# Layer 1's projection after its sums over edges instead of before them

## The chip, the cores and the metric

The kernel runs on one core of one Trainium2 chip. The metric is the time of one execution on the device in microseconds (us); the time before is the median of 14 runs. Engines are named as in the profile: PE is TensorE's matmul, PEld its weight load, DVE VectorE, ACT ScalarE, POOL GpSimd, SP SyncE. A line such as L589 is line 589 of the kernel before.

## The reference: what is computed

Two graph attention layers, each with a residual and a layer norm, over 3327 nodes of 1024 features. The adjacency matrix is symmetric, has ones on its diagonal and is sparse (each off-diagonal pair is drawn with a chance of 0.0024 in either direction).

```python
# layer 0: 8 heads of 128
h = x @ W0
e = leaky_relu(alpha_src[:, :, None] + alpha_dst[:, None, :], 0.2)   # per head
attn = softmax(where(adj == 0, -inf, e))
x = layernorm(x + concat_heads(attn @ h_heads))
# layer 1: one head of 1024
h = x @ W1
e = leaky_relu((h @ a1) + (h @ a2).T, 0.2)
attention = softmax(where(adj > 0, e, -9e15))
x = layernorm(x + relu(attention @ h))
```

All of it is float32.

## The kernel before, in words

Nodes are cut into 26 tiles of 128 targets (NT = 26). The kernel has a first stage and then one of two arms, chosen by a flag that the first stage computes; these inputs take the sparse arm.

**First stage (L320 to L441).** For each tile it loads rows of x and of the adjacency matrix, projects x with W0 (L415), computes the attention scores of layer 0 and writes a row of 1040 numbers for each node to DRAM (h0_d): 1024 projected features and 16 factors of the scores. It counts the edges and makes, for the first 13 tiles (LP = 13), lists of edges: for each of five blocks (EB = 5) four groups of 128 source indices (NG = 4, idx), a one-hot matrix of which of a group's 32 targets each edge belongs to (oh), and the targets' score factors (re). The lists of the other 13 tiles are made later, beside layer 0.

**Layer 0 in the sparse arm (class Layer0, L556 on).** A target tile has five steps. For each step `fetch` issues four indirect DMAs on POOL (`gather`, L513 to L521) that bring the rows of 4 x 128 edges from h0_d into one of five buffers (srcs, NS = 5). `fetch` of the next tile's step b is issued after step b of this tile, since it takes the same buffer; so gathers run a whole tile ahead. `step` makes the weights w (L580, L581) and the weighted one-hot matrices e (L583) on DVE, and sums over edges on PE: 32 matmuls of 128 columns, each for 32 targets (L589), and four small ones for the softmax's denominators (L597). A float32 matmul shows up as two records in the trace. `finish` divides, adds the residual, normalizes and stores the tile to x1_d (L612).

**Layer 1's projection (project1, L535 to L554)** is a generator: its parts are taken out one at a time by `fill`, which `step` calls after every second head, so they are written between the parts of the next tile's steps. It transposes the tile's output (eight transposes, L155, and two copies), multiplies with W1 (16 matmuls of 512 columns, L542), copies the sums to SBUF (L549), multiplies them with a1_src and a1_dst and adds up along the row (score1, L192), takes exponentials of the scores, and writes rows of 1028 numbers to h1_d (L553): 1024 features, a one, and three factors of the scores.

**Layer 1 in the sparse arm (class Target, L640 on, with Layer1, L445 on).** Again five steps a tile, with gathers of rows from h1_d. For each group, ACT (L654) and DVE (L658) make the weights es. PE sums the 1025 columns (1024 features and the one, whose sum is the denominator) in three cuts of 342, 342 and 341 columns (L664). `finish` (L462) applies the reciprocal and the Relu (L468), adds the residual, which `prepare` had loaded from x1_d (L454), normalizes and stores the output. It is called in step 2 of the next tile.

**What sets the order.** The program's order is a priority, not the order of execution: each engine's order is laid down when the program is built by a scheduler that lets later work go ahead where earlier work isn't ready by its own estimate. In the trace, L244, the start of an edge list, runs eight times between 633.7 and 709.0 us, though the program first asks for one of those lists eleven tiles later. On the chip each engine then works through its order strictly and waits at its head. Buffers are shared by tag: a tag with a number of slots hands out the next slot when its last reader is done.

```python
            while later:
                fill()
            la.finish()
```

In layer 0 this stands after the five steps of a tile (L633): what is left of the generators is written before the tile's finish, whose last line appends the tile's own projection for the next tile's steps.

Of the kernel before, what the change touches and what calls it, by code (L numbers as in the profile page):

```python
# [9 lines left out]
F32 = mybir.dt.float32  # L10
# [16 lines left out]
def kernel(  # L27
# [23 lines left out]


    nc = tc.nc
    N, D = x.shape
# [35 lines left out]
    h0_d = scratch.tile([NP, HW0], F32, name="h0_d")  # L90
    h1_d = scratch.tile([NP, HW], F32, name="h1_d")
    wd_d = [scratch.tile([P, WD], BF16, name=f"wd_d{t}") for t in range(NT)]
# [39 lines left out]
    def spread(dst, a):  # L132

        nc.sync.dma_start(dst, bass.AP(tensor=a.tensor, offset=a.offset, ap=[[0, P], [1, D]]))

    class Phase:
# [51 lines left out]
        def score1(self, ht, t):  # L188
# [6 lines left out]
            self.r1.weights(t)  # L195

        def load_a1(self):
            self.a1 = [self.pool.tile([P, D], F32, name=f"a1_{n}") for n in range(2)]
            spread(self.a1[0], a1_src)
            spread(self.a1[1], a1_dst)  # L200

# [243 lines left out]
    class Layer1:  # L445


        def __init__(self, ph, t):
            self.ph, self.t, self.src = ph, t, {}

        def prepare(self):
            self.r = self.ph.row(self.ph.r1, [self.t], 0)
            self.res = self.ph.sbuf("y", [P, D], 3, "res")
            nc.sync.dma_start(self.res, x1_d[self.t])  # L454

        def fetch(self, j):
            pass

# [15 lines left out]
    def layer1(targets, steps):  # L474
        targets[0].prepare()
        for j in range(steps):
            targets[0].fetch(j)
        for t, tg in enumerate(targets):
            tg.begin()
            for j in range(steps):  # L480
                tg.step(j)
                if t and j == min(3, steps // 2):
                    targets[t - 1].finish()
                if t + 1 < NT:
                    if j == steps // 2:
                        targets[t + 1].prepare()
                    targets[t + 1].fetch(j)
        targets[-1].finish()


    def sparse(own):
# [4 lines left out]
        for s in srcs:  # L496
            nc.vector.memset(s, 0.0)
        ph.r1 = Rows(pool, 1)
        wt = pool.tile([P, KT, D], F32, bufs=1, name="wt1")
        for k in range(KT):  # L500
            nc.sync.dma_start(wt[:, k, :], w1[k * P : (k + 1) * P, :])
        ph.load_a1()
        ph.edge_constants()
        later, listed = deque(), {}

# [28 lines left out]

        def project1(t, y):  # L535

            xT = sbuf("xT", [P, KT, P], 2)
            yield from ph.transposed(xT, y)
            acc = [bank("S", [P, HALF], "mm") for _ in range(2)]
            for k in range(KT):  # L540
                for g in range(2):
                    nc.tensor.matmul(  # L542
                        acc[g], xT[:, k, :], wt[:, k, g * HALF : (g + 1) * HALF], start=k == 0, stop=k == KT - 1
                    )
                yield
            ht = sbuf("x1", [P, HW], 2, "h1")
            nc.gpsimd.memset(ht[:, D : D + 1], 1.0)
            for g in range(2):
                nc.scalar.activation(ht[:, g * HALF : (g + 1) * HALF], acc[g], AF.Copy)  # L549
            ph.score1(ht[:, :D], t)  # L550
            for i, v in enumerate((ph.r1.a, ph.r1.b, ph.r1.nb)):
                nc.vector.tensor_copy(ht[:, D + 1 + i : D + 2 + i], v[:, t, :])
            nc.sync.dma_start(h1_d[t * P : (t + 1) * P, :], ht)  # L553
            yield  # L554

        class Layer0:  # L556
# [5 lines left out]
            def prepare(self):  # L562
                self.oh, self.re = listed.pop(self.t)
                self.ohf = sbuf("ohf", [P, NB, GT], 2)
                nc.scalar.activation(self.ohf, self.oh, AF.Copy)
                self.y = sbuf("y", [P, D], 3)
                load_rows(self.y, x, self.t)

# [33 lines left out]
            def finish(self):  # L602
                ri = sbuf("ri", [P, H], 2)
                nc.vector.reciprocal(ri, self.den)
                y = self.y
                for h in range(H):
# [4 lines left out]
                ph.layer_norm([y])  # L611
                nc.sync.dma_start(x1_d[self.t], y)  # L612
                later.append(project1(self.t, y))

# [6 lines left out]
        for b in range(EB):  # L621
            lays[0].fetch(b)
        for t, la in enumerate(lays):
            la.begin()
# [14 lines left out]

        class Target(Layer1):  # L640

            def prepare(self):
                super().prepare()
                self.oh = sbuf("oh", [P, NB, GT], 3, dt=U8)
                nc.sync.dma_start(self.oh, oh_d[self.t])

            def fetch(self, b):
                self.src[b] = gather(h1_d, HW, self.t, b)

            def step(self, b):  # L650
                s = self.src[b]
                es = sbuf("e", [P, NG, GT], 3, "es")
# [9 lines left out]
                for c in range(3):  # L662
                    for g in range(NG):
                        nc.tensor.matmul(  # L664
                            self.acc[c][g * GT : (g + 1) * GT, : CUTS[c + 1] - CUTS[c]], es[:, g, :],
                            s[:, g, CUTS[c] : CUTS[c + 1]], start=b == 0, stop=b == EB - 1,
                        )

        layer1([Target(ph, t) for t in range(NT)], EB)


# [149 lines left out]
```

## Time and profile before

| | |
|---|---|
| median of 14 runs | 2618.31 us (2603.04 to 2630.63) |
| the profiled execution | 2613.62 us |
| its span, first to last instruction | 2611.9 us |
| PE busy | 2022.8 us, 77% |
| DVE busy | 1143.6 us, 44% |
| ACT busy | 620.6 us, 24% |
| POOL busy | 1134.7 us, 43% |
| DMA | 611.67 MB, mean 234 GB/s |
| granted TensorE clock, mean | 0.854 |

The profile is a page about one execution. Its first part gives each engine's busy time; the second cuts the span into 40 slices of 65 us, with a digit of busy share for each engine, the clock that TensorE was granted and the DMA engines' share. Groups of instructions follow, by line, engine and operation, with their count, busy time, the mean time of one in nanoseconds, and the idle time of the engine just before them with what ended it. Further views answer questions on the trace: the timeline in order of time, windows (busy time of each engine between two instants), and the instructions of one line. A busy PE is not a PE at its peak, since records of pipelined matmuls overlap; "issue" is idle time in which the engine waited for nothing that the profile shows. Where shares of the whole span mix stages with different limits, windows tell them apart.

### The profile page before, as it was taken

To read this page: it belongs to the slowest core of one execution; us is meant where nothing else is said; L and a number is where in the kernel's file an instruction comes from. 1 tells how busy PE (TensorE), PEld (TensorE's weight loads), DVE (VectorE), ACT (ScalarE), POOL (GpSimd) and SP (SyncE) were. 2 spreads that over 40 slices of the span, in tenths; PEclk is the share of its full clock that TensorE was granted. 3 is DMA by queue.
4 is the path that set the end of the run, shared out by engine and by line. 5 is a ranking of instruction groups with operands and counts; after the bars stand their busy time and mean duration, and the time that the engine had idled before them with its cause. 6 is when DMAs were issued, how large, how long until landed. Compare 5 with 4: busy or idle time off the path is not lost. (4 is left out here: it accounts for less than half of the span.)

```text
span 2611.9 us, 44777 instructions
## 1 busy us (share of the span) xinstructions
PE 2022.8 (77%) x17161; PEld 1022.7 (39%) x17161; DVE 1143.6 (44%) x3188; ACT 620.6 (24%) x1478; POOL 1134.7 (43%) x1109
## 2 busy tenths in 40 slices
PE   3899879993788787878878787786867876777774
PEld 1444434442444444445445444542322332223221
DVE  6999761006733333357566553531222322223222
ACT  1333341110111111111111111111333333333331
POOL 0000000006454545455454544524666766666762
PEclk7899889995887887878878888787988998988987
DMA  5343562109777767777666776745999998999983
GB/s 173 94 112 96 119 135 81 57 34 367 257 250 257 267 237 266 243 242 250 221 238 231 247 252 215 246 144 201 342 346 343 334 349 308 355 326 337 336 319 139
DMA packets 199612, 611.67 MB, mean 234 GB/s; under 512 B 41588, under 2 KB 56564, under 8 KB 199392
## 3 DMA queue, kind: packets, MB, share of 16 engines
q0 software_dynamic: 153504, 492.33, 56.3%
q1 hardware_dynamic: 45888, 116.40, 12.2%
q8 instruction: 138, 2.26, 0.3%
q14 instruction: 82, 0.67, 0.1%
HBM read 651.88 MB, written 59.37 MB: 272 GB/s over the span
## 5 line engine op out<-in xcount | busy, mean ns | idle before, releaser
L516 POOL DMA_INDIRECT src<-h_d,idx x1040 | 1112.1, 1069 | 865.0 <-PE acc L589 372.0
L664 PE MATMUL acc<-src,es 128*32 128x342 f32 (+1 forms) x3120 | 580.7, 480 | 209.4 <-issue 144.1
L589 PE MATMUL acc<-src,e 128*32 128x128 f32 x8320 | 468.3, 331 | 106.9 <-issue 77.3
L664 PEld LDWEIGHTS acc<-src,es 128*32 128x32 f32 x3120 | 230.5, 114 | 549.3 <-issue 449.2
L589 PEld LDWEIGHTS acc<-src,e 128*32 128x32 f32 x8320 | 310.4, 131 | 291.8 <-issue 257.0
L415 PE MATMUL mm<-wt,xT 128*128 128x512 f32 x832 | 403.8, 626 | 12.9 <-DMA wt<-in_L_gnn_W_dram 12.9
L542 PE MATMUL mm<-wt,xT 128*128 128x512 f32 x832 | 387.3, 606 | 0.0
L654 ACT ACTIVATE es<-R,src 128x32 f32<-128x32 f32 x520 | 172.8, 403 | 212.1 <-PE acc L664 164.5
L415 PEld LDWEIGHTS mm<-wt,xT 128*128 128x128 f32 x832 | 154.6, 198 | 174.4 <-issue 153.6
L542 PEld LDWEIGHTS mm<-wt,xT 128*128 128x128 f32 x832 | 149.5, 191 | 162.6 <-issue 162.6
L658 DVE SCALAR_TENSOR_TENSOR es<-es,src,oh 128x32 f32<-128x32 f32 x520 | 121.5, 250 | 160.3 <-issue 93.9
L464 DVE RECIPROCAL ri<-acc 128x1 f32<-128x1 f32 x26 | 4.4, 168 | 390.2 <-remote 375.2
L129 POOL DMA_DIRECT2D ad<-in_adj_dram x26 | 14.2, 547 | 357.3 <-DVE ad L128 155.7
L192 DVE SCALAR_TENSOR_TENSOR pr<-h,a 128x1024 f32<-128x1024 f32 x52 | 63.7, 1225 | 221.9 <-ACT h L549 221.4
L583 DVE TENSOR_TENSOR e<-ohf,w 128x1024 f32<-128x1024 f32 x130 | 157.6, 1220 | 1.8
L597 PE MATMUL den<-w,ohf 128*32 128x8 f32 x1040 | 48.4, 191 | 129.2 <-DVE w L581 41.6
L549 ACT ACTIVATE h<-mm 128x512 f32<-128x512 f32 x52 | 31.0, 598 | 377.2 <-PE mm L542 242.1
L468 ACT ACTIVATE y<-acc,ri 128x342 f32<-128x342 f32 (+1 forms) x78 | 37.1, 543 | 281.4 <-issue 194.4
L340 ACT ACTIVATE junk<-ad 128x3328 bf16<-128x3328 bf16 x26 | 77.4, 2977 | 109.6 <-DVE ad L130 90.3
L597 PEld LDWEIGHTS den<-w,ohf 128*32 128x32 f32 x1040 | 41.1, 126 | 145.2 <-issue 107.9
L173 ACT ACT_TABLE_LOAD x50 | 64.2, 1283 | 66.9 <-DVE sg L172 51.3
L580 DVE TENSOR_TENSOR w<-src,re 128x32 f32<-128x32 f32 x130 | 23.3, 183 | 121.0 <-PE den L597 100.7
(116 smaller groups left out, 1656.7 us busy)
## 6 DMA issues: line engine op xcount, KB each, us to landing
ad<-in_adj_dram POOLq DMA_DIRECT2D x25, 831.8 KB
src<-h_d,idx POOLq DMA_INDIRECT x1040
h_d<-ht SPq DMA_DIRECT2D x26, 520.0 KB
h_d<-h SPq DMA_DIRECT2D x26, 514.0 KB
x_d<-y SPq DMA_DIRECT2D x26, 512.0 KB
res<-x_d SPq DMA_DIRECT2D x26, 512.0 KB
x<-in_x_dram SPq DMA_DIRECT2D x25, 512.0 KB
y<-in_x_dram SPq DMA_DIRECT2D x25, 512.0 KB
```

The costliest lines, as they stand in the source:

```text
L173: nc.scalar.activation(sg[:, 0, :nt], sg[:, 0, :nt], AF.Sqrt)
L192: nc.vector.scalar_tensor_tensor(pr, ht, 1.0, a, op0=OP.mult, op1=OP.mult, accum_out=self.r1.sd[:, t, n, :])
L340: nc.scalar.activation(junk, ad, AF.Copy, accum_out=deg)
L415: nc.tensor.matmul(acc[g], xT[t][:, k, :], wt[:, k, g * HALF : (g + 1) * HALF], start=k == 0, stop=k == KT - 1)
L516: nc.gpsimd.indirect_dma_start(out=s[:, g, :w], out_offset=None, in_=table[:, :], in_offset=bass.IndirectOffsetOnAxis(ap=idx[:, t, b * NG ...
L542: nc.tensor.matmul(acc[g], xT[:, k, :], wt[:, k, g * HALF : (g + 1) * HALF], start=k == 0, stop=k == KT - 1)
L583: nc.vector.tensor_tensor(e, self.ohf[:, blk, :].unsqueeze(2).to_broadcast([P, NG, H, GT]), w.unsqueeze(3).to_broadcast([P, NG, H, GT]), O ...
L589: nc.tensor.matmul(self.acc[h // 4][g * GT : (g + 1) * GT, h % 4, :], e[:, g, h, :], s[:, g, h * DH : (h + 1) * DH], start=b == 0 and h % ...
L597: nc.tensor.matmul(self.den[g * GT : (g + 1) * GT, :], self.ohf[:, b * NG + g, :], w[:, g, :], start=b == 0, stop=b == EB - 1,)
L654: nc.scalar.activation(es[:, g, :], self.r[:, 0, g * GT : (g + 1) * GT], AF.Relu, bias=s[:, g, D + 3 : D + 4], scale=s[:, g, D + 1 : D + 2],)
L658: nc.vector.scalar_tensor_tensor(es[:, g, :], es[:, g, :], s[:, g, D + 2 : D + 3], self.oh[:, b * NG + g, :], op0=OP.add, op1=OP.mult,)
L664: nc.tensor.matmul(self.acc[c][g * GT : (g + 1) * GT, : CUTS[c + 1] - CUTS[c]], es[:, g, :], s[:, g, CUTS[c] : CUTS[c + 1]], start=b == 0, ...
```

## The change: what it does

Sums over edges are linear, so weights times (rows times W1) equals (weights times rows) times W1. The kernel after gathers rows of layer 0's output, sums them with the attention weights, and multiplies each tile's sum with W1 afterwards. The scores need a1 and a2 applied to the projection, so W1 times a1 and W1 times a2 are computed once (score_weights), and each output row of layer 0 is multiplied with these two vectors.

- In layer 0, `finish` computes the two scores of the tile (two DVE products with a sum along the row), takes the exponentials and writes rows of 1028 numbers to y_d: the normalized features, a one and the three factors. project1 is no longer appended there. x1_d is no longer written.
- In layer 1, `gather` reads y_d. A step sums two cuts of 512 columns and one of a single column (the one, into a bank of its own). `fill` is called after each of the first two cuts.
- `finish` of a layer 1 tile applies the reciprocal, one half on ACT and one on DVE, loads the residual's rows from y_d, and appends project1, which transposes, multiplies with W1, applies the Relu, adds the residual, normalizes and stores the output. What is left of project1 after the next tile's steps is written ahead of that tile's finish, and after the last tile what is left of its own.
- score_weights runs once, between the first tile's gathers and its first step.

The diff, cut to its core:

```diff
+        def score_weights():
+            for n, a in enumerate((a1_src, a1_dst)):
+                av = sbuf("z", [P, D], 3, "av")
+                spread(av, a)
+                for k in range(KT):
+                    pr = sbuf("z", [P, D], 3, "pr")
+                    nc.vector.scalar_tensor_tensor(
+                        pr, wt[:, k, :], 1.0, av, op0=OP.mult, op1=OP.mult, accum_out=wc[:, n, k : k + 1]
+                    )
+                for g in range(2):
+                    tr = bank("T", [P, 4, P], "tr")
+                    for k in range(4):
+                        nc.tensor.transpose(
+                            tr[:, k, :], wc[:, n, 4 * g + k : 4 * g + k + 1].to_broadcast([P, P]), ident
+                        )
+                    nc.scalar.activation(wa[n][:, g * HALF : (g + 1) * HALF], tr.rearrange("p a b -> p (a b)"), AF.Copy)
...
-        def project1(t, y):
+        def project1(t, z, res):
...
-            yield from ph.transposed(xT, y)
+            yield from ph.transposed(xT, z)
...
-            ht = sbuf("x1", [P, HW], 2, "h1")
-            nc.gpsimd.memset(ht[:, D : D + 1], 1.0)
+            o = sbuf("z", [P, D], 3, "o")
             for g in range(2):
-                nc.scalar.activation(ht[:, g * HALF : (g + 1) * HALF], acc[g], AF.Copy)
-            ph.score1(ht[:, :D], t)
-            for i, v in enumerate((ph.r1.a, ph.r1.b, ph.r1.nb)):
-                nc.vector.tensor_copy(ht[:, D + 1 + i : D + 2 + i], v[:, t, :])
-            nc.sync.dma_start(h1_d[t * P : (t + 1) * P, :], ht)
+                nc.scalar.activation(o[:, g * HALF : (g + 1) * HALF], acc[g], AF.Relu)
+            nc.vector.tensor_tensor(o, o, res, OP.add)
+            ph.layer_norm([o])
+            n = rows(t)
+            nc.sync.dma_start(out[t * P : t * P + n, :], o[:n])
             yield
...
                 ph.layer_norm([y])
-                nc.sync.dma_start(x1_d[self.t], y)
-                later.append(project1(self.t, y))
+                for n in range(2):
+                    pr = sbuf("z", [P, D], 3, "pr")
+                    nc.vector.scalar_tensor_tensor(
+                        pr, y, 1.0, wa[n], op0=OP.mult, op1=OP.mult, accum_out=r1.sd[:, t, n, :]
+                    )
+                nc.gpsimd.memset(row[:, D : D + 1], 1.0)
+                nc.scalar.activation(row[:, D + 1 : D + 2], r1.d[:, t, :], AF.Exp)
+                nc.scalar.activation(row[:, D + 2 : D + 3], r1.d[:, t, :], AF.Exp, scale=SLOPE)
+                nc.vector.tensor_scalar(row[:, D + 3 :], row[:, D + 2 : D + 3], -1.0, None, op0=OP.mult)
+                nc.sync.dma_start(y_d[t * P : (t + 1) * P, :], row)
...
             def fetch(self, b):
-                self.src[b] = gather(h1_d, HW, self.t, b)
+                self.src[b] = gather(y_d, HW, self.t, b)
+
+            def begin(self):
+                self.acc = [bank("A", [P, HALF], "acc1") for _ in range(2)]
+                self.den = bank("D", [P, 1], "den1")
...
                 for c in range(3):
                     for g in range(NG):
+                        to = self.den if c == 2 else self.acc[c]
                         nc.tensor.matmul(
-                            self.acc[c][g * GT : (g + 1) * GT, : CUTS[c + 1] - CUTS[c]], es[:, g, :],
-                            s[:, g, CUTS[c] : CUTS[c + 1]], start=b == 0, stop=b == EB - 1,
+                            to[g * GT : (g + 1) * GT, :], es[:, g, :],
+                            s[:, g, c * HALF : min((c + 1) * HALF, D + 1)], start=b == 0, stop=b == EB - 1,
                         )
+                    if c < 2:
+                        fill()
+
+            def finish(self):
+                ri = sbuf("ri", [P, H], 2)
+                nc.vector.reciprocal(ri[:, :1], self.den)
+                z = sbuf("z", [P, D], 3)
+                nc.scalar.activation(z[:, :HALF], self.acc[0], AF.Copy, scale=ri[:, :1])
+                nc.vector.tensor_scalar(z[:, HALF:], self.acc[1], ri[:, :1], None, op0=OP.mult)
+                res = sbuf("y", [P, D], 3, "res")
+                nc.sync.dma_start(res, y_d[self.t * P : (self.t + 1) * P, :D])
+                later.append(project1(self.t, z, res))
+
+        targets = [Target(t) for t in range(NT)]
+        targets[0].prepare()
+        for b in range(EB):
+            targets[0].fetch(b)
+        for t, tg in enumerate(targets):
+            tg.begin()
+            for b in range(EB):
+                tg.step(b)
+                if t + 1 < NT:
+                    if b == EB // 2:
+                        targets[t + 1].prepare()
+                    targets[t + 1].fetch(b)
+            while later:
+                fill()
+            tg.finish()
+        while later:
+            fill()
```

## The prediction

> **What bounds the kernel now.** I read the page's slices first, since one busy share over the whole span mixes stages.
>
> ```profile
> PE   3899879993788787878878787786867876777774
> ...
> PEclk7899889995887887878878888787988998988987
> DMA  5343562109777767777666776745999998999983
> ```
>
> One digit is 65 us. From digit 11 on (layer 0's sums over edges) PE stands at 7 to 8 and DMA at 6 to 7; from digit 29 to 38 (layer 1's) DMA stands at 8 to 9. A target tile ends with a reciprocal (L604 in layer 0, L464 in layer 1), so their starts cut both stages into tiles: L604 from 648.8 to 1756.4, L464 from 1842.4 to 2582.5. The windows between them:
>
> ```profile
> core 0: us, PE busy (x) PEld busy (x) DVE busy (x) ACT busy (x) POOL busy (x), PEclk, DMA share, GB/s
> 648.80:1079.00 430.20, 346.24 (x4031) 186.59 (x4034) 182.59 (x481) 56.05 (x92) 220.25 (x210) 0.83 0.75 256
> 1079.00:1724.10 645.10, 518.40 (x6685) 316.00 (x6688) 348.52 (x998) 110.36 (x294) 324.14 (x299) 0.81 0.70 237
> ...
> 1842.40:2582.60 740.20, 555.09 (x3022) 222.86 (x3022) 205.62 (x701) 266.44 (x670) 494.33 (x484) 0.89 0.91 331
> ```
>
> Ten tiles of layer 0 take 43.0 us each; fourteen more, most of them with an edge list made beside them, 46.1; twenty-five of layer 1 take 29.6. Layer 1 is bound by its gathers: DMA share 0.91 at 331 GB/s. Layer 0 moves 256 x 430.2 / 10 = 11.0 MB a tile at a share of 0.75; it is bound by PE's serial work, which the timeline of one tile shows:
>
> ```profile
> 883.77 0.64 PE L589 MATMUL acc<-src,e 128*32 128x128 f32 x16
> 884.34 1.98 PE L542 MATMUL mm<-wt,xT 128*128 128x512 f32 x4
> 886.26 0.65 PE L589 MATMUL acc<-src,e 128*32 128x128 f32 x16
> ...
> 907.56 0.64 PE L589 MATMUL acc<-src,e 128*32 128x128 f32 x4 [0.78 <-issue]
> 908.98 1.09 PE L589 MATMUL acc<-src,e 128*32 128x128 f32 x5 [0.77 <-issue]
> ```
>
> The projection (L542) is woven into the first steps. At the tile's end short matmuls come four at a time, every 0.7 to 1.4 us, with the idle put down to "issue": PE waits for nothing the profile shows. From 901.6 to 911.9 that costs about 8 us.
>
> **The change, part by part.** Terms are made against the profiled execution: 2613.6 us, span 2611.9.
>
> *The projection leaves layer 0.* Its price:
>
> ```profile
> L664 PE MATMUL acc<-src,es 128*32 128x342 f32 (+1 forms) x3120 | 580.7, 480 | 209.4 <-issue 144.1
> ...
> L542 PE MATMUL mm<-wt,xT 128*128 128x512 f32 x832 | 387.3, 606 | 0.0
> ```
>
> 387.3 / 26 = 14.9 us of PE a tile, and 1.8 us of transposes (L155 on y: 45.7 / 26). Off DVE go a copy (0.69) and three small ones (0.45); off ACT a copy of xT (0.60) and two of the sums (0.60 each). The two score products (L192, 2 x 1.31) stay on DVE, but now in the finish, ahead of the next tile's w and e; nb waits there for two Exps behind a table load (1.28). So the gap at a tile's end (4.6 us before 1549.85) grows to about 9. What is late next: the gathers. They have five buffers, a whole tile, issued ahead, so a 9 us gap doesn't starve DMA. Lower bound: volume 11.0 MB less one of two written rows (0.5) is 10.5 MB, at layer 1's 331 GB/s 31.7 us. POOL needs 20 issues x 1.3 us = 26 us, below that; the new memset waits in that queue, and only the store of the row waits for it. Upper bound: tile 0, which has no projection beside it, keeps PE from 616.97 to 654.8, 37.8 us, with pulses of "issue" through it, but with DVE full of other work. I take 34.5, about the middle: DVE's load was tile 0's own, the pulses were not. Ten tiles: 430 - 345 = **-85**. For the fourteen, DVE has 348.5 / 14 = 24.9 us and PE the list's matmuls, which make the 3.1 us between 46.1 and 43.0 now; I add 2: 36.5 x 14 = 511, **-134**. The last tile has no gathers beside it and loses its projection: 32.3 to 20, **-12**.
>
> *Between the layers.* Layer 1's first gather waits for the last row in DRAM. Today the last tile's transposes and projection lie in that wait (1764.33 to 1782.2, then copies, store at 1786.1). They go, the scores stay: **-19**. They come back after the last sum, where nothing covers them: transposes 2.8, projection 15.1, copies about 1: **+19**.
>
> *The projection enters layer 1.* PE's work for a tile there: sums over edges now 60 matmuls of 342 columns, then 40 of 512 and 20 of one. Columns are nearly the same. The last tile, whose rows had landed, ran 70 records in 7.96 us (0.114 each), so 13.6 us for its 120; bounds are 10 (layer 0's 64 in 1.95 us, five steps) and 17.9 (99 records in 14.81 us at 1994.65, paced by gathers). One-column sums: not in the trace; the nearest row, eight columns (L597), is 1.9 a tile, and I take that. Projection 14.9, transposes 1.8, R's transpose 0.3. Weaving: 16 short and 4 long records take 2.49 us (883.77 to 886.26); unmixed, 16 of 64 in 1.95 are 0.49, and 4 of 24 in 10.47 (one piece, from 1556.50) 1.75. That is 0.25 a pair; with ten places to fill a tile 0 to 2.5, I take 1.5. Sum 34.0; with 1 for DVE and ACT, which execute in order and hold the next es behind the projection's Relu and norm, **35** (30.5 to 42.5). Gathers alone ask 29.6, so they no longer end last: 25 x (35 - 29.6) = **+135**. Starving for instructions I leave out: a tile then has some 320 PE and PEld instructions for layer 0's 806 now.
>
> The Trainium skill, "TensorEngine Tiling (Array Packing)", section Key Properties, says that changing the tiling mode drains TensorE, and this speaks against weaving 32-column sums with a 128-column projection. The row agrees in kind (0.25 us a pair); with a drain at all ten places the tile would be 36.0, with the projection in one piece 33.5.
>
> The row load for the residual moves from prepare to finish and is read some 30 us later; on SP it stands behind an output's store, and nothing on the path waits for it. The write of x1 disappears. Relu takes the place of two copies in kind.
>
> *score_weights.* 16 products of 1.31 us = 21 us of DVE once, after the weights land, ahead of layer 0. DVE idles there in pieces (4.7 us before 615.28, 6.2 before 588.77), and tile 0 needs the result only in its finish. Bounds 0 and 21: **+10**.
>
> Another page, "TensorE: Matmul & The Clock Gate", section HAM oscillation, says that idle gaps over about 3.4 us drop the clock to half. Here the clock was 0.77 between the layers, where PE waits long, against 0.83 and 0.89. A layer 0 with gaps would then run its sums at half speed, 20 us for 10, still under the gathers' 31.7; the sum stays.
>
> **Sum:** 2613.6 + 10 - 85 - 134 - 12 - 19 + 135 + 19 = 2527.6. The median shown, 2618.3, is 4.7 above the profiled execution: 2532.
>
> **Rivals.**
> *Both layers at the gathers' pace.* For it: layer 1's PE work is 34 only with waits and half clock counted in; at 0.114 and unwoven it falls towards 30. Layer 0 at 31.7 (-113) and 32 (-197), layer 1 at 30.6 (+25): 2613.6 + 10 - 113 - 197 - 12 + 25 + 4.7 = 2331. Against: PE and DMA would both be full with no loss between them. Chance 0.17.
> *Slower: layer 1 takes over layer 0's tile.* PE's work for a layer 1 tile becomes what layer 0's is now, and that takes 43.0, not 35; ACT and DVE, in order, wait for the projection and hold up the es of the next step. +335 in place of +135: 2732. It decides from 29.6 + 221 / 25 = 38.4 us a tile. Against: no eight DVE products at the tile's end, a third of the instructions. Chance 0.17.
> *Layer 0 does not fall.* The pulses of "issue" grow as short matmuls come closer together, and DVE binds where lists are made: 39 (-40) and 42 (-57): 2654. For it: tile 0. Chance 0.13.
> *It does not do what it says.* Each engine's order is the scheduler's: if a tile's projection stands in one piece where gathers don't run beside it, layer 1 takes 29.6 + 14.9 = 44.5: 2770. Against: five gathers stay issued. Chance 0.05.
>
> **The numbers.** My forecast, 2532, has 0.48 and its own range 2440 to 2620. Slower takes the second and fourth rival and half the third, 0.28; 0.3% (about 8 us) is what a measurement can tell from no change, and 0.05 lies within it; faster 0.67. The range runs from within the first rival to within the second, 2345 to 2725: it leaves out a part of each and the fourth.
>
> **What would show it.** Right: tiles of 32 to 37 us between layer 0's reciprocals with a DMA share near 0.9, tiles of 33 to 37 in layer 1 with a lower share than 0.91, projection rows only in layer 1's windows, the tail some 19 us longer. Wrong: "issue" idle growing in layer 0, or layer 1's es waiting behind the projection's Relu on ACT, with tiles past 38.4 us. If layer 1 stays at 30, PE's work there was overcounted.

## The result, and the profile after

The changed kernel takes **2876.04 us** (median of 10 runs, 2871.55 to 2879.46) where the kernel before takes 2618.05 beside it: ratio 1.098, 95% interval 1.096 to 1.100. It is 258 us slower; the forecast was 2532, and the range ended at 2725. The profiled execution's span is 2876.2 us, against 2611.9 before.

The slices of the changed kernel's page, one digit 72 us:

```profile
PE   3998889927566666666663799999999999999995
...
PEclk7999899966776676666766899999999999999998
DMA  5443641078888878877775866666666666666650
```

From digit 24 on, layer 1, PE is full, at full clock, and DMA has fallen to 6. The kernel before had it the other way round there. The windows of the three stages, cut at the reciprocals as before (ten tiles of layer 0, fourteen, twenty-five of layer 1):

```profile
core 0: us, PE busy (x) PEld busy (x) DVE busy (x) ACT busy (x) POOL busy (x), PEclk, DMA share, GB/s
667.48:998.19 330.71, 211.77 (x3588) 142.48 (x3579) 178.03 (x454) 39.86 (x69) 223.95 (x204) 0.70 0.86 311
998.19:1518.51 520.32, 336.74 (x6056) 243.33 (x6053) 336.87 (x934) 82.85 (x245) 317.20 (x294) 0.67 0.78 274
1625.02:2830.97 1205.95, 1175.32 (x4024) 387.12 (x4024) 245.30 (x751) 285.77 (x696) 480.27 (x484) 1.00 0.65 203
```

Layer 0 did about as forecast: a tile takes 33.1 and 37.2 us (34.5 and 36.5 were forecast), the DMA share is 0.86 and 0.78. Layer 1's tile takes 48.2 us, PE is busy for 47.0 of them, and the 25 tiles lie between 48.0 and 50.2: a fixed chain of PE work, not a race with the gathers. PE's timeline in one of those tiles (start, duration, engine, line, names, shapes, number of records):

```profile
2402.80 1.98 PE L553 MATMUL mm<-wt,xT 128*128 128x512 f32 x4
2404.71 1.90 PE L693 MATMUL acc<-src,es 128*32 128x512 f32 x4
2406.45 0.20 PE L693 MATMUL den<-src,es 128*32 128x1 f32 x2
2406.58 1.12 PE L553 MATMUL mm<-wt,xT 128*128 128x512 f32 x2
2407.64 1.90 PE L693 MATMUL acc<-src,es 128*32 128x512 f32 x4
2409.38 0.20 PE L693 MATMUL den<-src,es 128*32 128x1 f32 x2
2409.51 1.98 PE L553 MATMUL mm<-wt,xT 128*128 128x512 f32 x4
2411.42 1.92 PE L693 MATMUL acc<-src,es 128*32 128x512 f32 x8
```

L693 is the sum over edges, L553 the projection. A matmul is two records, so "x4" is one of a step's four groups: both halves of its 1024 columns for 32 targets. It takes 1.90 us; the "x8" below it, two groups side by side, takes 1.92. **Groups that stand together cost as much as one.** The program wrote all four groups side by side. The order laid down for PE has, in each tile, six groups alone and four pairs between pieces of the projection, and then six groups in a row at the tile's end. I took the reason to be that ACT and DVE make es group by group and a piece of the projection is ready in between; the first experiments test this.

Adding up the time from each record's start to the next one's, by line, over the 25 tiles splits the 48.2 us: sums over edges 28.0, one-column sums 3.2, projection 15.6, transposes 1.3. Of the 28.0 the six groups alone take 10.4, the four pairs 9.4 (not every pair runs as close as the one shown), and the six in a row 8.2.

| step of the sum | forecast | measured |
|---|---|---|
| start to layer 0's first reciprocal (648.8 to 667.5) | +10 | +18.7 |
| first ten tiles of layer 0 | -85 | -99.5 |
| next fourteen | -134 | -124.8 |
| last tile of layer 0 | -12 | +5.4 |
| between the layers | -19 | -17.3 |
| 25 tiles of layer 1 | +135 | +465.8 |
| tail | +19 | +15.9 |

### The profile page after: what moved, and what is told of

Same layout as the page of the kernel before. It is cut to its first block, busy times and chain, and to the rows that moved or that the text cites. A ratio compares the mean times of both kernels' runs of the same rounds, so it can differ in the third digit from the quotient of the medians.

```text
span 2876.2 us, 44684 instructions
## 1 busy us (share of the span) xinstructions
PE 2321.4 (81%) x17177; PEld 1067.3 (37%) x17177; DVE 1184.4 (41%) x3168; ACT 596.3 (21%) x1430; POOL 1132.9 (39%) x1109
## 5 line engine op out<-in xcount | busy, mean ns | idle before, releaser
L693 PE MATMUL acc<-src,es 128*32 128x512 f32 x2080 | 784.9, 604 | 34.9 <-DVE es L686 25.9
L527 POOL DMA_INDIRECT src<-y_d,idx x520 | 516.1, 992 | 727.1 <-PE den L693 536.5
L527 POOL DMA_INDIRECT src<-h_d,idx x520 | 591.6, 1138 | 349.2 <-PE acc L599 165.8
L599 PE MATMUL acc<-src,e 128*32 128x128 f32 x8320 | 531.0, 375 | 175.2 <-issue 120.4
L599 PEld LDWEIGHTS acc<-src,e 128*32 128x32 f32 x8320 | 367.5, 150 | 306.5 <-issue 238.7
L553 PE MATMUL mm<-wt,xT 128*128 128x512 f32 x832 | 421.6, 621 | 0.0
L411 PE MATMUL mm<-wt,xT 128*128 128x512 f32 x832 | 407.2, 631 | 11.0 <-DMA wt<-in_L_gnn_W_dram 11.0
L693 PEld LDWEIGHTS acc<-src,es 128*32 128x32 f32 x2080 | 163.6, 109 | 493.1 <-issue 434.2
L693 PEld LDWEIGHTS den<-src,es 128*32 128x32 f32 x1040 | 96.5, 110 | 253.7 <-issue 253.7
L682 ACT ACTIVATE es<-R,src 128x32 f32<-128x32 f32 x520 | 174.5, 402 | 35.2 <-issue 10.4
L553 PEld LDWEIGHTS mm<-wt,xT 128*128 128x128 f32 x832 | 138.7, 190 | 82.3 <-issue 78.9
L559 ACT ACTIVATE o<-mm 128x512 f32<-128x512 f32 x52 | 31.0, 597 | 361.9 <-PE mm L553 361.9
L693 PE MATMUL den<-src,es 128*32 128x1 f32 x1040 | 89.3, 170 | 1.0 <-issue 1.0
```

The costliest lines, as they stand in the source:

```text
L411: nc.tensor.matmul(acc[g], xT[t][:, k, :], wt[:, k, g * HALF : (g + 1) * HALF], start=k == 0, stop=k == KT - 1)
L527: nc.gpsimd.indirect_dma_start(out=s[:, g, :w], out_offset=None, in_=table[:, :], in_offset=bass.IndirectOffsetOnAxis(ap=idx[:, t, b * NG ...
L553: nc.tensor.matmul(acc[g], xT[:, k, :], wt[:, k, g * HALF : (g + 1) * HALF], start=k == 0, stop=k == KT - 1)
L559: nc.scalar.activation(o[:, g * HALF : (g + 1) * HALF], acc[g], AF.Relu)
L599: nc.tensor.matmul(self.acc[h // 4][g * GT : (g + 1) * GT, h % 4, :], e[:, g, h, :], s[:, g, h * DH : (h + 1) * DH], start=b == 0 and h % ...
L682: nc.scalar.activation(es[:, g, :], self.r[:, 0, g * GT : (g + 1) * GT], AF.Relu, bias=s[:, g, D + 3 : D + 4], scale=s[:, g, D + 1 : D + 2],)
```

## The experiments

Three theories go through them. **A**: the sums are dear because groups of 32 columns stand one at a time between projection matmuls. **B**: ACT and DVE work in order, and es waits there behind the projection's Relu and norm. **C**: the projection's own time and the changes between 32-column and 128-column matmuls fill PE. Kernels sent together shared a chip and its runs of the kernel before; ratios are to those, so they are to be compared across groups with care. In the first two groups and the last the kernel before took 2642 to 2652 us.

### First group: the order of the groups

**e1_together** makes es of all four groups in two DVE operations, so that four groups come ready at once:

```diff
-                    nc.vector.scalar_tensor_tensor(
-                        es[:, g, :], es[:, g, :], s[:, g, D + 2 : D + 3], self.oh[:, b * NG + g, :],
-                        op0=OP.add, op1=OP.mult,
-                    )
+                nc.vector.tensor_tensor(es, es, s[:, :, D + 2 : D + 3].to_broadcast([P, NG, GT]), OP.add)
+                nc.vector.tensor_tensor(es, es, self.oh[:, b * NG : (b + 1) * NG, :], OP.mult)
```

> The changed kernel, with layer 1's weights es finished for all four groups of a step by two DVE operations on 128 x 128 (add, multiply by the one-hot matrix) in place of four on 128 x 32, so that the four groups become ready together and PE's order has the four 32-column matmuls of a cut in a row. Theory A (32-column groups that PE works through one at a time, with pieces of the projection between them, leave three quarters of the array idle): five steps of 4 x 0.43 us and the small ones are 9.5 us, with projection 13.7, transposes and switches some 5, so PE needs about 28 us a tile and the gathers end last again; tiles of 30 to 32 us in place of 48.2, total 2420 to 2500. Theory B (es stands on ACT behind the projection's Relu and PE waits for it): ACT's order keeps both, tiles stay above 44 us, total above 2770. Theory C (the projection's own time and the changes between 32 and 128 columns fill PE): the same work is left, total above 2770.

**e4_group_by_group** has the same two operations, but the matmuls are written group after group with a piece of the projection behind each:

```diff
-                for c in range(3):
-                    for g in range(NG):
+                for g in range(NG):
+                    for c in range(3):
...
-                    if c < 2:
+                    if g < NG - 1:
                         fill()
```

> As e1_together, es of the four groups ready at once, but the matmuls written group by group (the loop over groups outside that over cuts) with a fill behind each of the first three groups. Theory A: PE again has one group of 32 columns at work between pieces of the projection, tiles of 44 to 49 us, total 2770 to 2900. Theory B: es is ready early as in e1_together, so the time would be that of e1_together under B. Theory C: as the changed kernel, 2850 to 2900. Between A and C e1_together decides; this run shows that the order alone, with the same operations, brings the loss back.

Measured: e1 2541.82 us, ratio **0.962** (0.961 to 0.964), layer 1's tile 34.3. e4 2910.63 us, ratio **1.103** (1.100 to 1.107), tile 49.1. Both have the same instructions; between them lies only the order in which the program writes them. PE's timeline in e1 and then in e4:

```profile
2203.14 1.92 PE L691 MATMUL acc<-src,es 128*32 128x512 f32 x16
2204.88 0.22 PE L691 MATMUL den<-src,es 128*32 128x1 f32 x8
2205.03 5.42 PE L553 MATMUL mm<-wt,xT 128*128 128x512 f32 x12
2210.37 1.92 PE L691 MATMUL acc<-src,es 128*32 128x512 f32 x16
```

```profile
2402.10 1.98 PE L553 MATMUL mm<-wt,xT 128*128 128x512 f32 x4
2404.02 1.90 PE L691 MATMUL acc<-src,es 128*32 128x512 f32 x4
2405.76 0.20 PE L691 MATMUL den<-src,es 128*32 128x1 f32 x2
2405.89 0.32 PE L184 MATMUL tr<-ident,sd 128*128 128x128 f32 x1
2406.05 1.02 PE L553 MATMUL mm<-wt,xT 128*128 128x512 f32 x2
2407.00 1.90 PE L691 MATMUL acc<-src,es 128*32 128x512 f32 x4
```

Sixteen records in 1.92 us, or four in 1.90. With es made at once PE's order has the four groups side by side, so the reason given above holds. And this shows A: the sums take 28.0 us a tile in e4, as in the changed kernel, and 11.7 in e1. C falls too. e1 has the whole projection in the same tile and takes 14 us less. It also has fewer changes between the two kinds of matmul, four pieces of projection a tile in place of ten, but the traces give their price: a piece of 2, 4 or 12 records takes 1.06, 1.91 or 5.35 us up to the next sum, which is 0.43 a record and 0.2 for the piece. That makes 1.2 of the 14 us. e1's tile still missed the 30 to 32 that A gave; the second group looks at what is left.

**e2_piece** puts the projection in one piece behind the sums, with es still made group by group; **e3_before_together** gives the kernel before the two operations.

```diff
-                    if c < 2:
-                        fill()
...
-            while later:
-                fill()
             tg.finish()
+            while later:
+                fill()
```

> The changed kernel, with no fill inside a step of layer 1: a tile's projection is written whole right behind its finish, ahead of the next tile's steps. The es operations stay as they are, one group at a time. Theory A: no piece of the projection stands between groups, so the four column groups overlap at least in the steps behind the projection: 13.7 + 1.5 + 12 to 20 us of sums, tiles of 30 to 36 us, total 2420 to 2570. Theory B: the Relu still stands ahead of es on ACT and comes still earlier, total above 2770. Theory C: the switches go (at most 3 us a tile), total 2790 to 2850.

> The kernel before, with the same two DVE operations in place of four per step in layer 1. All theories: its layer 1 waits for gathers, so nothing changes, 2600 to 2630; more than that would say that the new operations are a gain by themselves.

Measured: e2 2794.79 us, ratio 1.058 (1.056 to 1.060), tile 44.2; e3 2686.51 us, ratio **1.018** (1.014 to 1.022), tile 31.7, where the kernel before has 29.6 in its trace from another chip.

e2 missed what A gave, 30 to 36, and landed where B and C had it. Its sums did fall, from 28.0 to 14.7 us a tile, as A says; what takes their place is shown with e8 below.

e3 missed too: in the kernel before, making es together costs time. PE's idle time before L662 is put down to "issue" for 417.5 us, against 144.1 before. One reading is that the first matmul of a step now waits for all four gathers. The trace doesn't show it: 337 of the 417.5 us lie in 25 stretches in which no matmul record stands and PE's semaphore counts on all the same (more on them at the end of this section), and the cause stays open. So the two operations are no gain by themselves, and e4, which has them and is slower than the changed kernel, says the same: e1's gain isn't a cheaper es, but the order of PE's work behind it.

### Second group: what is dear, and what is left in e1

**e6_no_projection** is the changed kernel without the projection's transposes and matmuls:

```diff
-            yield from ph.transposed(xT, z)
-            acc = [bank("S", [P, HALF], "mm") for _ in range(2)]
-            for k in range(KT):
...
-                nc.scalar.activation(o[:, g * HALF : (g + 1) * HALF], acc[g], AF.Relu)
+                nc.scalar.activation(o[:, g * HALF : (g + 1) * HALF], z[:, g * HALF : (g + 1) * HALF], AF.Relu)
```

> The changed kernel with layer 1's projection left out: no transposes of z, no matmuls with the weights, Relu taken on z itself; es and its one-group-at-a-time order of the 32-column matmuls stay. What is tested: whether that order alone is dear, or only with projection matmuls between the groups. Theory A (the four groups overlap only where their matmuls follow each other on PE): with nothing between them the sums fall from 28 us a tile to 12 to 16, layer 1's tile is back at the gathers' pace, 29 to 32 us, and the time is 2400 to 2480. Rival (512 columns in place of 342 make the group-by-group order dear by itself): the sums stay at 25 us or more, the tile at 33 to 38 with the one-column sums and waits, time 2500 to 2620. Theory C (projection's own time and mode changes): tile 30 with the sums still near 28 us.

Measured: 2454.65 us, ratio 0.928 (0.923 to 0.933), tile 31.1. PE's order is still group by group:

```profile
2205.64 1.05 PE L685 MATMUL acc<-src,es 128*32 128x512 f32 x4
2206.50 0.20 PE L685 MATMUL den<-src,es 128*32 128x1 f32 x2
2206.53 1.06 PE L685 MATMUL acc<-src,es 128*32 128x512 f32 x6
```

With nothing in between the next group starts 0.89 us after the last (2205.64 to 2206.53): its first half overlaps the second half of the one before. That is 17.8 us for a tile's twenty groups (18.9 when all 25 tiles are added up), above the 12 to 16 that A gave, below the rival's 25. The DMA share is 0.87, near the 0.91 of the kernel before, so these sums hide behind the gathers. Four together cost 0.48 a group, group after group 0.89, one alone between projection matmuls 1.90.

**e8_together_piece** joins e1 and e2. **e7_more_small** issues e1's one-column matmuls three times, to see whether the number of instructions limits PE. **e5_scores_later** moves e1's score_weights to where tile 0 first needs it.

```diff
-                        to = self.den if c == 2 else self.acc[c]
+                        if c == 2:
+                            for k in range(3):
+                                nc.tensor.matmul(
+                                    self.den[g * GT : (g + 1) * GT, k : k + 1], es[:, g, :],
+                                    s[:, g, D : D + 1], start=b == 0 and k == 0, stop=b == EB - 1 and k == 2,
+                                )
+                            continue
```

```diff
-        score_weights()
         for t, la in enumerate(lays):
...
             while later:
                 fill()
+            if t == 0:
+                score_weights()
             la.finish()
```

> e1_together with the projection of a tile in one piece behind its sums, so that nothing stands between the quartets and es of the next tile is behind the projection on ACT. If mode changes and the mixing cost PE what e1_together still lies over the gathers' pace, the tile falls from 34.3 to 30 to 33 us, time 2440 to 2510. If a piece stops the sums and the gathers behind it (as e2_piece, 44.2 us a tile against 48.2 mixed), PE's work is about 27 us but stands in line with waits: tile 36 to 42, time 2580 to 2740. No difference: 2530 to 2555.

> e1_together with each one-column matmul of layer 1 issued three times (into three columns of the denominator, the first is used): 40 more matmuls a tile, 80 more records, and no more columns to speak of. A tile of e1_together is 34.3 us with PE busy 29.2. If PE's limit is time in the array, 80 records of 0.05 us are 4 us, part of it in PE's idle time: tile 34 to 38, time 2545 to 2640. If the supply of instructions limits PE (8 instructions, 4 weight loads and 4 matmuls, in 0.72 us, as in the stretches of 'issue'), 160 more instructions are up to 14 us: tile 44 to 48, time 2780 to 2880.

> e1_together with score_weights moved from ahead of layer 0's first tile to just ahead of its finish. In the changed kernel the first reciprocal of layer 0 came 18.7 us later than in the kernel before, where the forecast had 10. If DVE's products ahead of the first es are what makes it late, the first reciprocal goes back to 650 to 658 us and the time falls by 5 to 15 us from e1_together (ratio to the kernel before about 0.957 to 0.961). If it is the sums of the weights on PE and ACT, or the later landing of something else, the reciprocal stays at 668 and the ratio at 0.962.

Measured: e8 2770.23 us, ratio 1.044 (1.042 to 1.047), tile 43.3; e7 2582.88, ratio 0.974 (0.972 to 0.977), tile 35.9; e5 2529.94, ratio **0.955** (0.951 to 0.959), first reciprocal at 649.8.

e7: 160 more records a tile (80 matmuls, 80 weight loads) cost 1.6 us; their number is not the limit in e1. e5: the 18.7 us at the start were score_weights, whose products stand on DVE ahead of tile 0's first w and again ahead of its second e. All but 1 us of them come back (the repeat below has its first reciprocal at 653.9). Its first ten tiles of layer 0 take 5 us longer than e1's, which ran on another chip.

e8 has its groups in fours, and the tile is still 9 us longer than e1's, a little past the 36 to 42 that its second case gave. PE is busy for 32.3 of the 43.3 us. Its timeline, and windows over the projection and over the rest of that tile:

```profile
2303.37 15.14 PE L553 MATMUL mm<-wt,xT 128*128 128x512 f32 x32
2318.43 1.92 PE L691 MATMUL acc<-src,es 128*32 128x512 f32 x16
...
2333.31 3.58 PE L691 MATMUL acc<-src,es 128*32 128x512 f32 x13 [4.99 <-ACT es L682]
...
2342.31 1.11 PE L156 MATMUL tr<-ident,z 128*128 128x128 f32 x4 [3.51 <-ACT z L700]
```

```profile
2303.37:2318.43 15.06, 15.06 (x33) 6.33 (x32) 1.75 (x6) 3.93 (x11) 0.99 (x1) 0.92 0.08 28
2318.43:2342.31 23.88, 14.22 (x123) 5.10 (x122) 5.88 (x13) 7.85 (x18) 15.34 (x15) 0.88 0.89 327
```

The last two numbers of a window are the DMA share and GB/s. While the projection stands in one piece the gathers stand still (0.08, 28 GB/s), and then PE waits while they catch up (0.89, 327 GB/s). A gather needs a buffer that a sum has freed, and no sum runs in the piece: POOL's gathers wait on PE's one-column sums for 429.6 us in the 25 tiles of e8, for 230.8 in e1. Over all 25 tiles the DMA share in the piece is 0.16 in e8 and 0.08 in e2. So the projection and the gathers add up instead of running side by side: 15.7 us of projection and 27.6 of the rest in e8, 14.0 and 30.2 in e2. The woven form has a use, then: the sums between its pieces free buffers, and the gathers go on (DMA share 0.84 in e1's layer 1, 0.61 in e2's and e8's). The waits in brackets, for es and z, are where the lost time shows on PE; PE's semaphore counts on in 38 of e8's 39 gaps of over 2 us.

What is left in e1 over the gathers' 29.6 is a stop. The timeline in e1's tile, of PE and then of ACT and DVE, and windows around it:

```profile
2212.26 1.13 PE L553 MATMUL mm<-wt,xT 128*128 128x512 f32 x2
2217.10 3.97 PE L691 MATMUL acc<-src,es 128*32 128x512 f32 x16 [3.71 <-issue]
```

```profile
2213.43 0.60 ACT L559 ACTIVATE o<-mm 128x512 f32<-128x512 f32 x1 [2.05 <-PE mm L553]
2213.92 1.01 ACT L682 ACTIVATE es<-R,src 128x32 f32<-128x32 f32 x3
...
2214.06 1.23 DVE L560 TENSOR_TENSOR o<-o,res 128x1024 f32<-128x1024 f32 x1 [9.53 <-ACT o L559]
2215.32 0.69 DVE L171 BATCH_NORM_STATS2 st<-o 128x6 f32<-128x512 f32 x1
2215.93 0.27 DVE L686 TENSOR_TENSOR es<-es,src 128x128 f32<-128x128 f32 x1
2216.12 0.68 DVE L171 BATCH_NORM_STATS2 st<-o 128x6 f32<-128x512 f32 x1
2216.72 0.27 DVE L687 TENSOR_TENSOR es<-es,oh 128x128 f32<-128x128 f32 x1
```

```profile
2203.10:2215.60 12.50, 10.29 (x63) 3.85 (x62) 2.09 (x4) 4.13 (x11) 7.56 (x9) 1.00 0.93 330
2215.60:2225.85 10.25, 7.66 (x44) 4.07 (x44) 4.74 (x13) 3.04 (x8) 5.17 (x6) 0.50 0.93 321
2225.85:2237.20 11.35, 11.35 (x63) 4.57 (x55) 1.21 (x4) 4.41 (x11) 7.14 (x8) 1.00 0.75 233
```

The page calls the stop "issue", but the lines of ACT and DVE name the cause: es for the last step is finished at 2217.0, and it stood on ACT behind the projection's Relu, then on DVE behind its residual and norm statistics. That is theory B, a stop of 3.7 us in most tiles (2.99 in two). Behind the stop the granted clock (third from the end) is 0.50 for 10.25 us, and the same sixteen records take 3.97 us. The Trainium skill's page "TensorE: Matmul & The Clock Gate", section HAM oscillation, says that an idle gap over some 3.4 us halves the clock. The 3.71 us stop agrees in kind, but the traces don't show 3.4 as the limit: here the half clock starts 2.2 us into the stop, the two stops of 2.99 us brought it too, and in e10 below the clock falls to 0.50 for 3.41 us twelve times with no gap of over 1.2 us ahead of it. It holds for 10.24 us behind 18 of e1's 25 stops; the first five tiles have it twice for 3.41.

### Third and last group: the order on ACT and DVE

**e10_norm_next_tile** is e5 with the projection taken two matmuls deeper at each place and its Relu, residual and norm taken up in the next tile. **e11_norm_only** does this alone to the changed kernel.

```diff
-                yield
+                if k % 2 == 1:
+                    yield
+            for _ in range(4):
+                yield
             o = sbuf("z", [P, D], 3, "o")
...
             nc.sync.dma_start(out[t * P : t * P + n, :], o[:n])
-            yield
...
-            while later:
-                fill()
             tg.finish()
```

> e5_scores_later with the projection taken two matmuls deeper at each place, so that it is through in the first half of a tile, and its Relu, residual and norm taken up in the next tile's first step, when its matmuls are long done; nothing is left out. A tile of e5_scores_later is 34.3 us: about 27 of PE's work at full clock, a stop of 3.7 in which es stands on ACT behind the projection's Relu and on DVE behind its norm, and some 10 us after each stop at a granted clock of 0.5. If that order is what is left over the gathers' pace: no stop over 3 us, clock over 0.95 in layer 1, tile 29.6 to 31.5, DMA share 0.9 or more, time 2410 to 2460, ratio to the kernel before 0.914 to 0.928. If the stop is the gathers' own (a late landing) or mode changes: tile 33.5 to 35, ratio 0.95 to 0.96.

> The changed kernel with this later Relu and norm alone: es is made group by group as in the changed kernel, and score_weights stays where it was. The fourth corner of a square: changed kernel (neither mended), e1_together (groups together), e10 (both). Theory B alone (ACT's and DVE's order): tile 48.2 down to 30 to 36 us, time 2420 to 2570. Theory A (the groups stand apart on PE): PE stays full. In this kernel's order the groups stand apart in steps 0 to 2 (some 13 of 1.72 to 1.94 us less than the halves that pair up, about 15 us) and follow each other in steps 3 and 4 (about 2.3 us a step): sums 19 to 21 us in place of 28, tile 38 to 41, time 2630 to 2710, ratio to the kernel before 1.0 to 1.025.

Measured on a chip where the kernel before takes 2361.27 us: e10 2226.97, ratio 0.942 (0.939 to 0.945), tile 29.5; e11 2634.04, ratio 1.116 (1.112 to 1.119), tile 45.4, with PE busy for 43.2 of it and sums of 24.2. That its ratio is worse than the changed kernel's comes from the kernel before, which is faster on this chip; the tile is 2.9 us shorter. B alone repairs 3 us of the tile, A alone 14. My 38 to 41 for e11 was too low, mostly in the sums, 24.2 for 19 to 21: the eight groups that follow each other took 6.8 for 4.6, the others 17.4 for some 15.

That chip moved 355 GB/s in layer 0 of e10, where e5 moved 308 on its chip, so I put the changed kernel, e5 and e10 on one chip:

> The changed kernel once more, on one chip with e13 and e14. Its layer 1 tile is PE's own work at full clock, so 47 to 49 us on any chip. Where the kernel before takes some 2630 us: ratio 1.09 to 1.105, layer 0 tiles 33 and 37. Where it takes some 2360 (faster gathers, layer 0 tiles 28 and 30): the kernel before gains in both layers, this one only in layer 0: 2690 to 2720, ratio 1.13 to 1.155.

> e5_scores_later once more. If its layer 1 tile is set by the stop in ACT's and DVE's order and the half clock behind it, it is 33.5 to 35 us on any chip: ratio 0.95 to 0.96 where the kernel before takes 2630, 0.985 to 1.005 where it takes 2360. If it is set by gathers, the tile falls to 28 to 31 on the faster chip, ratio 0.93 to 0.95.

> e10_norm_next_tile once more. Layer 1 tile 29.5 us on the faster chip, 29.5 to 31.5 on the others, with no stop of PE over 3 us and a clock over 0.95 in layer 1: 0.035 to 0.055 below e13 on either; ratio 0.94 where the kernel before takes 2360, 0.912 to 0.928 where it takes 2630. If the later norm were worth nothing, e13 and e14 would be within 0.01.

Measured, the kernel before at 2648.85: changed kernel 2890.41, ratio **1.092** (1.089 to 1.094), tile 48.2; e5 2529.51, ratio **0.955** (0.952 to 0.959), tile 34.2; e10 2660.79, ratio **1.005** (1.004 to 1.007), tile 39.8. The first two came as expected. e10, for which 29.5 to 31.5 was forecast, did not: the same kernel has a tile of 29.5 us on one chip and 39.8 on the other. The end of a tile, in e10 on its first chip and then in its repeat:

```profile
1976.75 2.25 PE L694 MATMUL acc<-src,es 128*32 128x512 f32 x16 [0.39 <-ACT es L685]
1978.46 0.57 PE L694 MATMUL den<-src,es 128*32 128x1 f32 x8
1980.15 0.66 PE L156 MATMUL tr<-ident,z 128*128 128x128 f32 x4 [1.12 <-ACT z L705]
```

```profile
2248.03 2.25 PE L694 MATMUL acc<-src,es 128*32 128x512 f32 x16 [0.39 <-ACT es L685]
2249.74 0.57 PE L694 MATMUL den<-src,es 128*32 128x1 f32 x8
2259.68 1.12 PE L156 MATMUL tr<-ident,z 128*128 128x128 f32 x4 [9.37 <-issue]
```

The records are alike up to the last sum; then the second has a stop of 9.37 us. In it PE's semaphore still counts up, about every 1.4 us, so the matmuls aren't done where their records stand. **The cause is open.** The kernel before, e2, e3, e6, e8 and e10's repeat have such a stretch (a gap of over 2 us between records in which PE's semaphore counts on at least twice) at least about once a layer 1 tile; in all of them steps of sums follow each other with no projection between, and in the stretches the DMA share is 0.89 to 1.01. e1 and e5 have at most five in all, e7 nine, the changed kernel none behind its first tile. But e10 on its first chip, in the same order, has none there either. No run here tells whether e5 beats the kernel before on that chip; where both ran, e5 beats both kernels.

## Why the prediction was wrong

**The step that failed** is the first term of layer 1's tile: "The last tile, whose rows had landed, ran 70 records in 7.96 us (0.114 each), so 13.6 us for its 120; bounds are 10 ... and 17.9". It measured 28.0, which is 14.4 us more; the whole tile missed its 35 by 13.2. The row was from a tile with nothing but sums, where each group overlaps the next; all three of my rows were. The change puts projection matmuls between the groups, and then a group costs 1.90 us alone. The same order without the projection costs 17.8 (e6), about my upper bound; the groups in fours take 11.7 in e1, a stretch at half clock included, and 9.1 in e10 at nearly full clock. I had counted columns and assumed that overlap belongs to the instruction. It belongs to the neighbours.

The Trainium skill's page "TensorEngine Tiling (Array Packing)", section Key Properties, says that tiles work independently and in parallel, beside the drain that I cited. The trace shows this only for tiles that stand together in PE's order. I priced mixing by its drain, 1.5 us, and not by the lost overlap. The row that I took the price from could not show the loss: its sixteen short records at 883.77 are two heads of four groups each, side by side.

Not all of the 28.0 is lost overlap. The six groups in a row at a tile's end take 8.2 us, where e6's pace gives 5.3: there es comes late, behind the projection's residual and norm on DVE. By these two numbers B's share is some 3 us, an estimate, and e11 gained 2.9.

The other terms of the tile: projection 15.6 for 14.9, one-column sums 3.2 for 1.9, transposes 1.3 for 2.1. Weaving, at 1.5, came nearly as worked: ten pieces a tile at 0.2 each are 2.0, and they stand in the projection's 15.6, which is 13.9 in one piece (e2). The range of the tile doesn't follow from its terms, though: they add up to 29.9 and 40.3, not to 30.5 and 42.5.

**What held.** Layer 0 fell by what was forecast (-224 together for -219, with a DMA share of 0.86 where it was 0.75), though by luck so closely: the ten tiles missed by 14.5 one way and the fourteen by 9.2 the other. The wait between the layers (-17.3 for -19) and the tail (+15.9 for +19) came out as worked. score_weights cost 18.7 of the 21 that could be: I took the middle, but its products stood ahead of tile 0's own work on DVE. The last tile of layer 0 rose by 5.4 where I had -12: I called it free of gathers, but its own now land late; DVE waits 6.4 and 8.9 us for them.

**The rivals.** The slower rival came true in direction only: the tile passed its 38.4 us and its 43.0 too, but not since "ACT and DVE, in order, wait for the projection and hold up the es". PE itself was full, by the groups' order. That wait exists, some 3 us of the changed kernel's tile and a stop of 3.7 in e1's; what its removal brings once the order is mended isn't shown, since e10 ran with e5 on one chip only, and was slower there. Of "It does not do what it says" the first half came true: the program's side-by-side groups were not what PE was given. Its case, a projection in one piece beside which no gathers run, isn't what the changed kernel does, but its 44.5 us is what that costs: e2 has 44.2, e8 43.3. (Ahead of the prediction I named L244 as an example of the scheduler's freedom: it runs seven times between 633.7 and 709.0 us, not eight.) My argument against the slower case, a third of the instructions, was the wrong measure: in e7 160 more records cost 1.6 us.

## What to carry to other kernels

When long matmuls are woven between short column groups that share the array, price the groups one by one, not by a row where they stand side by side, and look at the order that the scheduler lays down before trusting the order in the program. Operands that became ready one at a time made this scheduler split such groups; making those of all groups at once kept them together, and turned +9.2% into -4.5% with score_weights moved too. The same edit cost 1.8% where gathers set the pace (e3), so look first at what ends last. Don't take the long matmuls out of the weave for it: in one piece they held the buffers that the gathers needed, and the tile took the time of both (e2, e8).

## What the runs showed of the hardware beyond this

- Column groups: one group of 2 x 512 columns takes 1.90 us, four side by side 1.92, group after group 0.89 each.
- A piece of projection woven between groups costs 0.2 us beside its records, in pieces of 2 to 12 records.
- A stop of 3.71 us in a loop brought a granted clock of 0.50 for 10.25 us in most of e1's tiles. PE was busy for 7.66 us of that window, so by this number the half clock cost some 3.8 us, an estimate, as much again as the stop. In e10 two gaps of 1.1 and 0.8 us with four transposes between them, at 1508.2, were followed by 3.41 us at 0.50.
- Chips differ: the kernel before took 2361 us on one and 2618 to 2652 on the others, and one and the same kernel (e10) was 6% faster than it on the first and not faster on another.
- In some stretches PE's semaphore counts up long after the records of its matmuls end (to 2258.7 us where the last record starts at 2250.1). Where DVE's wait there is called "remote", the records are not to be trusted to the microsecond.
